# Keeping the loaded x tiles for the residual, and a new order of steps in the first part of an adaLN block

## The chip, the cores and the metric

The kernel runs on one core of a Trainium2 chip. The metric is the device time of one execution in microseconds (us), lower is better. A core has a matrix engine (TensorE, PE in the profile), a vector engine (VectorE, DVE), a scalar engine (ScalarE, ACT), a general engine (GpSimd, POOL) and a sync engine (SyncE, SP), which here does nothing but issue DMAs. Each engine works through its own queue of instructions in order; semaphores tie the queues together. Products are made in PSUM, everything else lies in SBUF.

## The reference, cut to what matters

```python
mod = (silu(c) @ wmod).reshape(2, 6, 1, 512)          # c: (2, 512)
sa, ca, ga, sb, cb, gb = mod[:, 0], ..., mod[:, 5]     # ga, gb: magnitude at least 0.25
h = layernorm(x) * (1 + ca) + sa                       # x: (2, 4096, 512) float32
x = x + ga * attn(h, W_qkva, gamma)                    # first part
h = layernorm(x) * (1 + cb) + sb
x = x + gb * ffn(h, w_gate, w_up, w_down)              # second part

def attn(x, W, gamma):
    xn = x / norm(x) * sqrt(512) * gamma
    q, kv, a = split(xn @ W.T, 3)                      # each (2, 4096, 512)
    y[n] = sigmoid(a[n]) * y[n-1] + kv[n]              # a scan along the tokens
    return q * y

def ffn(x, wg, wu, wd):                                # Q: blockwise FP4 quantize and dequantize
    h = silu(Q(x) @ Q(wg).T) * (Q(x) @ Q(wu).T)        # 1408 wide
    return Q(h) @ Q(wd).T
```

## The kernel before

**Tiling.** 8192 tokens make 64 tiles of 128 rows (index `g`) and 16 blocks of 512 tokens (index `i`), four tiles to a block. The first part (the attention-like half) writes `x + ga * attn` to the output in DRAM; the second part reads it back and adds the feed-forward half.

**The first part in slots.** There are 64 working slots. Slot `slot = 4 i + e` multiplies block `i` with the 128 output channels `e` of `q`, `kv` and `a`: 3 groups of 12 matmuls (L385) into three PSUM banks; two slots' banks alternate. The order in which each engine meets the steps of a slot is written out by hand, in one loop under a manual schedule. Beside the products of slot `s`, a slot does:

- the chain of slot `s-1`'s products: `gates` (the sigmoid on ScalarE, L403, and in the kernel before the DMA load of the matching x channels, `xs`, L398), `scan` on VectorE (L410), `read_out` on VectorE (L417 copies the last column for the next block, L419 multiplies by q), `halves` (ScalarE splits the result into 16-bit halves `yh`, L426, and SyncE issues their DMA transpose to `yt`, L428);
- for slot `s-2`: `joined` (ScalarE puts the transposed halves together, L434) and `residual` (GpSimd adds `xs`, L441, and issues the store, L443);
- the norm of x tiles ahead: the load of tile `s+7` (L328), the moments and `rstd` of tile `s+6` (L151, L156, L158, and the power on GpSimd, L159), center, shift, square and gain of tile `s+5` (L163, L169, L346, L351, L353), and the rounding into a high and a low half of tile `s+4` (`norm_hi`, L359, on ScalarE, and `norm_lo`, L364, on VectorE) with the DMA transpose into `xT` (L368), of which the next block's products are made;
- one or two units of the feed-forward weights: in the maxima slots (`max`, `maxd`, about slots 6 to 22) two block maxima with small steps (L145, L467, L472, L473); then one `finish`, in which GpSimd reduces the maxima over all partitions (L477) and VectorE takes the reciprocal (L478); then in 34 quantizing slots one unit, the generator `quant`, whose steps `advance(0)` to `advance(6)` are spread over the slot (L101, L107, L109, L120, L123, L125, L127 on VectorE, L103, L113, L116, L118 on ScalarE, and a transpose issued by SyncE).

The tiles named `ld` (8 buffers) hold loaded x tiles and loaded weight rows; center and shift work in place in them.

**Around it.** Before the slots, `start()` loads the modulation and projection weights; slots 0 to 3 also prepare the projection weights. From slot 58 on, four tiles of the first part's result are loaded (L557) and the first two are normed and quantized for the second part (`stats_x`, `quant_x`). The second part (L838, L853, L858, L888 and the same `quant`) begins when the last slot's products are through.

Of the kernel before, what the change touches and what calls it, by code (L numbers as in the profile page):

```python
# [8 lines left out]
F32 = mybir.dt.float32  # L9
F16 = mybir.dt.float16  # L10
BF16 = mybir.dt.bfloat16
U16 = mybir.dt.uint16
# [9 lines left out]
B = 2  # L22
# [22 lines left out]
def tile_adaln_block(  # L45
# [108 lines left out]
    def mean_rstd(st):  # L154
        mv = small.tile([P, 2], F32, name="mv", tag="mv", bufs=5)
        V.bn_aggr(mv, st)  # L156
        rstd = small.tile([P, 1], F32, name="rstd", tag="rstd", bufs=5)
        V.tensor_scalar(rstd, mv[:, 1:2], 1e-5, None, ALU.add)  # L158
        G.tensor_tensor(rstd, rstd, mhalf[:, 0:1], ALU.pow)  # L159
        return mv[:, 0:1], rstd  # L160

    def center(xt, mean, scale):
        V.scalar_tensor_tensor(  # L163
            out=xt, in0=xt, scalar=mean, in1=scale, op0=ALU.subtract, op1=ALU.mult
        )
        return xt

    def shift(h, rstd, by):
        V.scalar_tensor_tensor(out=h, in0=h, scalar=rstd, in1=by, op0=ALU.mult, op1=ALU.add)  # L169
# [2 lines left out]
        return work.tile([P, 2, D], F16, name="hl", tag="hl", bufs=4)  # L172

    def load_tile():
        return work.tile([P, D], F32, name="ld", tag="ld", bufs=8)


    pa = ExitStack()
# [71 lines left out]
        )  # L250

    def mod_store(s, pm):
        row = apool.tile([B, D], F32, name="row", tag="sig", bufs=2)
        if s == 5:
            signed_floor(row, pm, apool.tile([B, D], F32, name="mag", tag="y", bufs=3))
        else:
            A.activation(row, pm, AF.Copy, bias=1.0 if s in (1, 4) else 0.0)
        G.dma_start(modd[s], row)
# [61 lines left out]

    PARTS = (2, 1, 0)

    xld, xstat, xh = {}, {}, {}

    def norm_load(g):
        xld[g] = load_tile()
        b, t0 = divmod(g * P, N)
        S.dma_start(xld[g], x[b, t0 : t0 + P, :])  # L328

    def norm_moments(g):  # L330
        xstat[g] = moments(xld[g])

    def norm_stats(g):
        xstat[g] = mean_rstd(xstat[g])

    def norm_center(g):
        xh[g] = center(xld.pop(g), xstat[g][0], ca[g * P // N])

    def norm_shift(g):
        shift(xh[g], xstat.pop(g)[1], sa[g * P // N])  # L340
# [5 lines left out]
        A.activation(sq, h, AF.Square, accum_out=ss)  # L346
        xh[g] = h, ss

    def norm_gain(g):
        h, ss = xh[g]  # L350
        V.tensor_scalar(ss, ss, 1e-24, 1.0 / (D * XGAIN * XGAIN), ALU.max, ALU.mult)  # L351
        rn = small.tile([P, 1], F32, name="rn", tag="rn")
        G.tensor_tensor(rn, ss, mhalf[:, 0:1], ALU.pow)  # L353
        xh[g] = h, rn
# [38 lines left out]
        return i, e, ps  # L393

    def gates(i, e, ps):
        b, t0 = divmod(i * TB, N)
        xs = apool.tile([P, KC, P], F32, name="xs", tag="xs", bufs=3)
        S.dma_start(  # L398
            xs,
            x[b, t0 : t0 + TB, e * P : (e + 1) * P].rearrange("(t p) d -> p t d", p=P),  # L400
        )
        sig = apool.tile([P, TB], F32, name="sig", tag="sig", bufs=2)
        A.activation(sig, ps[0], AF.Sigmoid, scale=us[:, e, 2:3])  # L403
        return i, e, ps, xs, sig

    def scan(i, e, ps, xs, sig):
        b = i // BPB
        y = apool.tile([P, TB], F32, name="y", tag="y", bufs=3)
        init = 0.0 if i % BPB == 0 else carry[e]
        V.tensor_tensor_scan(out=y, data0=sig, data1=ps[1], initial=init, op0=ALU.mult, op1=ALU.add)  # L410
        return i, e, ps, xs, y

    def read_out(i, e, ps, xs, y):
        b = i // BPB
        if i % BPB != BPB - 1:
            cy = small.tile([P, 1], F32, name="cy", tag="cy", bufs=8)
            V.tensor_copy(cy, y[:, TB - 1 : TB])  # L417
            carry[e] = cy
        V.scalar_tensor_tensor(  # L419
            out=y, in0=ps[2], scalar=gq[:, e, b : b + 1], in1=y, op0=ALU.mult, op1=ALU.mult  # L420
        )
        return i, e, xs, y

    def halves(i, e, xs, y):
        yh = apool.tile([P, 2, TB], U16, name="yh", tag="yh", bufs=2)
        A.copy(yh, y.bitcast(U16).rearrange("p (t h) -> p h t", h=2))  # L426
        yt = apool.tile([P, 2, KC, P], U16, name="yt", tag="yt", bufs=2)
        S.dma_start_transpose(  # L428
            yt.rearrange("p h t e -> p (h t) e"), yh.rearrange("p h t -> p (h t)")
        )  # L430
        return i, e, xs, y, yt

    def joined(i, e, xs, y, yt):
        A.copy(  # L434
            y.bitcast(U16).rearrange("p (t e h) -> p t e h", t=KC, h=2),
            yt.rearrange("p h t e -> p t e h"),
        )
        return i, e, xs, y

    def residual(i, e, xs, y):  # L440
        G.tensor_tensor(xs, xs, y.rearrange("p (t e) -> p t e", t=KC), ALU.add)  # L441
        b, t0 = divmod(i * TB, N)
        G.dma_start(  # L443
            out[b, t0 : t0 + TB, e * P : (e + 1) * P].rearrange("(t p) d -> p t d", p=P), xs
        )
# [275 lines left out]
        mod_store(*r0)  # L721

    units, coming = [], []
    gate = joining = rows = None
    NS = NBLK * KC
    plan = [[]] * (KC + 1) + plan
    order = tc.manual_schedule(engines={V.engine, A.engine, G.engine, S.engine, T.engine})
    with order:
        xT = new_xT()
        start()  # L730
        for slot in range(NS + 2):
            i, e = divmod(slot, KC)
            if e == 0 and slot < NS:
                if slot:
                    xT = nxT
                nxT = new_xT() if i + 1 < NBLK else None
# [12 lines left out]
            if 0 < slot < 3:  # L749
                for part in PARTS:  # L750
                    hi_qkva(slot + 1, part, False)
                    lo_qkva(slot + 1, part)
            if gate is not None:
                gate = gates(*gate)
            for u in units:
                u.advance(0)
            if g < NT:
                norm_hi(g)
            if slot < 2:
                for part in PARTS:  # L760
                    gamma_qkva(slot + 2, part)
                    square_qkva(slot + 2, part)
            if gate is not None:
                gate = scan(*gate)
            for u in units:
                u.advance(1)
            if g + 1 < NT:
                norm_center(g + 1)
            if slot == 1:
                signed_floor(gq, cols, atile([P, KC, B], F32, "mag"))  # L770
                prep_gain(0)
            if gate is not None:
                gate = read_out(*gate)
            if g < NT:
                norm_lo(g, nxT)
            if g + 1 < NT:
                norm_shift(g + 1)
            for u in units:
                u.advance(2)
            if joining is not None:  # L780
                residual(*joined(*joining))
            joining = halves(*gate) if gate is not None else None
            if g + 1 < NT:
                norm_square(g + 1)
            for u in units:
                u.advance(3)
            if g + 2 < NT:
                norm_moments(g + 2)
            for u in units:
                u.advance(4)  # L790
            if g + 2 < NT:
                norm_stats(g + 2)
            for u in units:
                u.advance(5)
            if g + 1 < NT:
                norm_gain(g + 1)
            for u in units:
                u.advance(6)
            if slot < 2:
                scale_qkva(slot + 2)  # L800
            if 0 < slot < KC:
                prep_gain(slot)
            if i == 0 and e < 3:
                load_mod(3 + e)
            if late is not None:
                mod_store(*late)
            if slot == KC + 1:
                ca[1] = mod_load(1, 1, "mod_c1")
# [193 lines left out]
```

## Time and profile before

| | |
|---|---|
| median of 3 runs | 1994.95 us (1994.4 to 1995.38) |
| the profiled execution's own time | 1995.35 us |
| its span in the profile | 1993.6 us |
| busy PE, DVE | 1924.2 us (97%), 1669.2 us (84%) |
| busy ACT, POOL | 986.3 us (49%), 352.3 us (18%) |
| projection matmuls (L385), first to last | 29.0 to 609.4 us |
| residual add (L441) | 64 times, mean 1437 ns |
| second loads of x (`xs`) | 64 of 256 KB |

The profile is of one execution. Lines such as L169 are lines of the kernel before. A line of the timeline has the start in us, the duration in us, the engine, the line, the operation, what it writes and reads with shapes, and in brackets how long the engine was idle before it and what ended that. Neighbouring VectorE records overlap by some 0.08 us, so the distance of two starts is the better measure of what an instruction costs.

### The profile page before, as it was taken

What the parts mean: (1) busy time and instruction counts of PE and PEld (TensorE: products, weight loads), DVE (VectorE), ACT (ScalarE), POOL (GpSimd) and SP (SyncE); (2) the same over time, 40 slices, a digit from 0 to 9 for tenths busy, and PEclk for the clock granted to TensorE, in tenths of its full rate; (3) what the DMA queues carried; (4) which work ended last, traced back from release to release, by engine and by line L of the source; (5) the groups of instructions that cost most, each with busy time, mean ns of one, the idle gap of its engine ahead of it and who ended that gap; (6) DMA issues with size and microseconds to landing.
All of it is one profiled execution on the core that took longest, in us unless ns stands there. A gap on an engine that the chain in (4) does not pass through costs nothing.

```text
span 1993.6 us, 25757 instructions
## 1 busy us (share of the span) xinstructions
PE 1924.2 (97%) x9253; PEld 908.9 (46%) x9253; DVE 1669.2 (84%) x2851; ACT 986.3 (49%) x1648; POOL 352.3 (18%) x479
## 2 busy tenths in 40 slices
PE   7999979899989999999999999999999999999997
PEld 4344434344334444444444444444444444444444
DVE  5799979999965998888888888888888888888873
ACT  4444456666664554444444444444444444444431
POOL 4433334333331110000000000000000000000000
PEclk8999989999999999999999999999999999999999
DMA  8898879989963343433433433433533533433423
GB/s 246 210 240 217 197 167 218 209 207 205 206 166 78 67 88 68 82 65 66 83 65 66 83 65 76 83 66 70 81 69 62 85 66 64 84 67 62 80 46 50
DMA packets 516640, 222.98 MB, mean 112 GB/s; under 512 B 440470, under 2 KB 474518, under 8 KB 516512
## 3 DMA queue, kind: packets, MB, share of 16 engines
q1 hardware_dynamic: 501872, 187.76, 43.4%
q0 software_dynamic: 14640, 33.58, 9.7%
q8 instruction: 72, 1.18, 0.2%
q14 instruction: 56, 0.46, 0.1%
HBM read 79.43 MB, written 33.57 MB: 57 GB/s over the span
## 4 chain that ended last, share of the span: by engine, by line
PE 67%; DVE 19%; issue 7%; DMA 3%; POOL 1%; ACT 1%; SPq 0%; DVEq 0%; POOLq 0%; ACTq 0%
PE mm L838 41%; PE sd L888 21%; PE mm L385 4%; DVE ld L169 3%; DVE y L410 2%; DVE hl L364 2%; DVE ld L163 1%; DVE st L151 1%; DMA scratch<-in_L_wmod_dram 1%; DVE xn L120 1%; DVE hl L123 1%; DVE xn L107 1%; DVE y L419 1%; DMA yt<-yh 1%; DMA xT<-hl 1%
## 5 line engine op out<-in xcount | busy, mean ns | idle before, releaser
L838 PEld LDWEIGHTS <-x2T 128*128 128x128 f16 x4608 | 450.9, 98 | 470.5 <-issue 2.2
L385 PE MATMUL mm<-xT,wqT 128*128 128x512 f16 (+1 forms) x2412 | 516.0, 377 | 43.4 <-DMA xT<-hl 36.3
L838 PE MATMUL mm<-wuT,x2T 128*128 128x512 f16 (+1 forms) x2304 | 487.7, 361 | 2.0 <-DVE hid L858 2.0
L838 PE MATMUL mm<-wgT,x2T 128*128 128x512 f16 (+1 forms) x2304 | 487.7, 361 | 0.0
L888 PE MATMUL sd<-wdT,hT 128*128 128x512 f16 (+1 forms) x2145 | 469.0, 378 | 5.0 <-DMA hT<-hhl 5.0
L385 PEld LDWEIGHTS <-wqT 128*128 128x128 f16 x2412 | 232.7, 99 | 328.3 <-issue 72.8
L888 PEld LDWEIGHTS <-hT 128*128 128x128 f16 x2145 | 211.2, 99 | 246.3 <-DMA hT<-hhl 5.5
L853 ACT ACTIVATE silu<-mm,u 128x512 f32<-128x512 f32 (+1 forms) x192 | 124.9, 650 | 293.1 <-PE mm L838 292.9
L858 DVE SCALAR_TENSOR_TENSOR hid<-mm,u,silu 128x512 f32<-128x512 f32 (+1 forms) x192 | 128.5, 672 | 147.0 <-PE mm L838 137.1
L569 POOL TENSOR_SCALAR rstd<-vs 128x1 f32<-128x1 f32 x64 | 14.3, 224 | 984.7 <-ACT sq L567 984.7
L141 ACT ACTIVATE u<-ud,rms 128x1 f32<-128x1 f32 x64 | 18.9, 295 | 278.4 <-DVE rms L137 278.4
L113 ACT ACTIVATE she<-sh 128x512 bf16<-128x512 bf16 (+2 forms) x162 | 148.7, 918 | 4.1
L118 ACT ACTIVATE sle<-sl 128x512 f16<-128x512 f32 (+2 forms) x162 | 147.0, 907 | 0.0
L441 POOL TENSOR_TENSOR xs<-xs,y 128x512 f32<-128x512 f32 x64 | 91.9, 1437 | 207.5 <-ACT y L434 207.5
L359 ACT ACTIVATE hl<-ld,rn 128x512 f16<-128x512 f32 x64 | 46.2, 722 | 132.7 <-POOL rn L353 131.8
L911 POOL DMA_DIRECT2D out_dram<-o x65 | 57.3, 881 | 282.6 <-DVE o L908 278.8
L120 DVE SCALAR_TENSOR_TENSOR xn<-hid,xn 128x1408 f32<-128x1408 f32 x64 | 103.6, 1618 | 3.7 <-ACT hid L116 3.7
L107 DVE TENSOR_TENSOR xn<-hid,inv 128x1408 f32<-128x1408 f32 x64 | 104.0, 1625 | 2.2
L123 DVE SCALAR_TENSOR_TENSOR hhl<-hid,xn 128x1408 f16<-128x1408 f32 x64 | 104.0, 1625 | 2.2
L145 DVE TENSOR_REDUCE amh<-hid 128x88 f32<-128x1408 f32 x64 | 103.7, 1620 | 2.2
L116 ACT ACTIVATE hid<-xn 128x1408 f32<-128x1408 f32 x64 | 88.2, 1378 | 30.9 <-DVE xn L107 30.9
L169 DVE SCALAR_TENSOR_TENSOR ld<-ld,rstd,mod 128x512 f32<-128x512 f32 x96 | 96.2, 1002 | 6.8 <-DVE ld L577 0.5
(109 smaller groups left out, 1887.6 us busy)
## 6 DMA issues: line engine op xcount, KB each, us to landing
ld<-in_L_attn_x_dram SPq DMA_DIRECT2D x64, 256.0 KB, 3.7
xs<-in_L_attn_x_dram SPq DMA_DIRECT2D x64, 256.0 KB, 4.0
out_dram<-xs POOLq DMA_DIRECT2D x64, 256.0 KB, 4.4
ld<-out_dram SPq DMA_DIRECT2D x64, 256.0 KB, 2.9
out_dram<-o POOLq DMA_DIRECT2D x63, 256.0 KB, 3.9
ld<-in_L_ffn_w_gate_dram SPq DMA_DIRECT2D x22, 256.0 KB, 4.3
ld<-in_L_ffn_w_up_dram SPq DMA_DIRECT2D x22, 256.0 KB, 3.7
scratch<-in_L_wmod_dram SPq DMA_DIRECT2D x4, 1024.0 KB, 6.1
```

The source lines that it names most:

```text
L107: V.tensor_tensor(blocks(xn), blocks(src), spread(inv, nb), ALU.mult)
L113: A.activation(blocks(she), spread(sh, nb), AF.Copy, scale=WPEAK)
L118: A.activation(blocks(sle), spread(sl, nb), AF.Copy, scale=WPEAK)
L120: V.scalar_tensor_tensor(out=xn, in0=a, scalar=FLOOR, in1=xn, op0=ALU.max, op1=ALU.add)
L123: V.scalar_tensor_tensor(out=nq, in0=a, scalar=FLOOR, in1=xn, op0=ALU.max, op1=ALU.subtract)
L145: V.tensor_reduce(am, src.rearrange("p (b k) -> p b k", k=QB), AX.X, ALU.max, apply_absolute_value=True)
L169: V.scalar_tensor_tensor(out=h, in0=h, scalar=rstd, in1=by, op0=ALU.mult, op1=ALU.add)
L385: T.matmul(pp[:, t : t + width], wqT[:, wp * KC + k, r * P : (r + 1) * P], xT[:, xp * KC + k, t : t + width], start=n == 0, stop=n == 3 * ...
L838: T.matmul(pp[:, : n1 - n0], x2T[:, xp * KC + k, :], wt[:, wp * KC + k, n0:n1], start=n == 0, stop=n == 3 * KC - 1,)
L853: A.activation(sl[:, :w], pairs[j][0][:, :w], AF.Silu, scale=u[:, 0:1])
L858: V.scalar_tensor_tensor(out=hid[:, n0:n1], in0=pairs[j][1][:, : n1 - n0], scalar=u[:, 1:2], in1=sl[:, : n1 - n0], op0=ALU.mult, op1=ALU.mult,
L888: T.matmul(pd, hT[:, hp * IC + k, :], wdT[:, wd_chunk(wp, k), d : d + width], start=n == 0, stop=n == 3 * IC - 1,)
```

## The change

The loaded x tiles go into a buffer of their own, one tile `xr` for the four x tiles of a block (4 buffers), and stay there: center writes its result into a fresh `ld` tile (7 buffers instead of 8), and the residual adds the result into a slice of `xr` and stores that. The second load of x goes. `sig` and `yh` have one buffer instead of two. The addition ahead of the power for `rstd`, and in the slots the step L351 of `norm_gain`, move from VectorE to GpSimd; the copy of the last column moves from VectorE to ScalarE. `joined` and `residual` come one slot later and at the head of the slot, ahead of scan and read-out in program order; `halves` follows the read-out at once; moments and `rstd` come before the weight unit's `advance(1)`; center, shift, square and gain stand together after `advance(2)`, and `advance(3)` to `advance(6)` follow them without a break. One more slot drains the queue of joined results.

```diff
-        V.tensor_scalar(rstd, mv[:, 1:2], 1e-5, None, ALU.add)
+        G.tensor_scalar(rstd, mv[:, 1:2], 1e-5, None, ALU.add)
...
     def center(xt, mean, scale):
+        h = load_tile()
         V.scalar_tensor_tensor(
-            out=xt, in0=xt, scalar=mean, in1=scale, op0=ALU.subtract, op1=ALU.mult
-        )
-        return xt
+            out=h, in0=xt, scalar=mean, in1=scale, op0=ALU.subtract, op1=ALU.mult
+        )
+        return h
...
-        return work.tile([P, D], F32, name="ld", tag="ld", bufs=8)
+        return work.tile([P, D], F32, name="ld", tag="ld", bufs=7)
...
     def norm_load(g):
-        xld[g] = load_tile()
+        i, t = divmod(g, KC)
+        if i not in xrows:
+            xrows[i] = apool.tile([P, KC, D], F32, name="xr", tag="xr", bufs=4)
+        xld[g] = xrows[i][:, t, :]
...
-    def norm_gain(g):
+    def norm_gain(g, engine=V):
         h, ss = xh[g]
-        V.tensor_scalar(ss, ss, 1e-24, 1.0 / (D * XGAIN * XGAIN), ALU.max, ALU.mult)
+        engine.tensor_scalar(ss, ss, 1e-24, 1.0 / (D * XGAIN * XGAIN), ALU.max, ALU.mult)
...
     def gates(i, e, ps):
-        xs = apool.tile([P, KC, P], F32, name="xs", tag="xs", bufs=3)
-        S.dma_start(
-            xs,
-            x[b, t0 : t0 + TB, e * P : (e + 1) * P].rearrange("(t p) d -> p t d", p=P),
-        )
-        sig = apool.tile([P, TB], F32, name="sig", tag="sig", bufs=2)
+        sig = apool.tile([P, TB], F32, name="sig", tag="sig", bufs=1)
...
-            V.tensor_copy(cy, y[:, TB - 1 : TB])
+            A.copy(cy, y[:, TB - 1 : TB])
...
-        yh = apool.tile([P, 2, TB], U16, name="yh", tag="yh", bufs=2)
+        yh = apool.tile([P, 2, TB], U16, name="yh", tag="yh", bufs=1)
...
-    def residual(i, e, xs, y):
+    def residual(i, e, y):
+        xs = xrows[i][:, :, e * P : (e + 1) * P]
         G.tensor_tensor(xs, xs, y.rearrange("p (t e) -> p t e", t=KC), ALU.add)
...
-        for slot in range(NS + 2):
+        for slot in range(NS + 3):
...
                 u.advance(0)
+            if len(joining) == 2 or slot >= NS + 2:
+                residual(*joined(*joining.pop(0)))
             if g < NT:
                 norm_hi(g)
...
                 gate = scan(*gate)
-            for u in units:
-                u.advance(1)
-            if g + 1 < NT:
-                norm_center(g + 1)
...
-                gate = read_out(*gate)
+                joining.append(halves(*read_out(*gate)))
+            if g + 2 < NT:
+                norm_moments(g + 2)
+                norm_stats(g + 2)
+            for u in units:
+                u.advance(1)
             if g < NT:
                 norm_lo(g, nxT)
-            if g + 1 < NT:
-                norm_shift(g + 1)
             for u in units:
                 u.advance(2)
-            if joining is not None:
-                residual(*joined(*joining))
-            joining = halves(*gate) if gate is not None else None
             if g + 1 < NT:
+                norm_center(g + 1)
+                norm_shift(g + 1)
                 norm_square(g + 1)
-            for u in units:
-                u.advance(3)
-            if g + 2 < NT:
-                norm_moments(g + 2)
-            for u in units:
-                u.advance(4)
-            if g + 2 < NT:
-                norm_stats(g + 2)
-            for u in units:
-                u.advance(5)
-            if g + 1 < NT:
-                norm_gain(g + 1)
-            for u in units:
-                u.advance(6)
+                norm_gain(g + 1, G)
+            for n in range(3, 7):
+                for u in units:
+                    u.advance(n)
```

More of the change, by code (lines that the diff above doesn't have):

```diff
@@ L252, in mod_store @@
     def mod_store(s, pm):
-        row = apool.tile([B, D], F32, name="row", tag="sig", bufs=2)
+        row = apool.tile([B, D], F32, name="row", tag="sig", bufs=1)
         if s == 5:
@@ L321, in tile_adaln_block @@
     PARTS = (2, 1, 0)
-    xld, xstat, xh = {}, {}, {}
+    xld, xstat, xh, xrows = {}, {}, {}, {}
     def norm_load(g):
-        xld[g] = load_tile()
+        i, t = divmod(g, KC)
+        if i not in xrows:
+            xrows[i] = apool.tile([P, KC, D], F32, name="xr", tag="xr", bufs=4)
+        xld[g] = xrows[i][:, t, :]
         b, t0 = divmod(g * P, N)
@@ L395, in gates, with scan @@
     def gates(i, e, ps):
-        b, t0 = divmod(i * TB, N)
-        xs = apool.tile([P, KC, P], F32, name="xs", tag="xs", bufs=3)
-        S.dma_start(
-            xs,
-            x[b, t0 : t0 + TB, e * P : (e + 1) * P].rearrange("(t p) d -> p t d", p=P),
-        )
-        sig = apool.tile([P, TB], F32, name="sig", tag="sig", bufs=2)
+        sig = apool.tile([P, TB], F32, name="sig", tag="sig", bufs=1)
         A.activation(sig, ps[0], AF.Sigmoid, scale=us[:, e, 2:3])
-        return i, e, ps, xs, sig
-    def scan(i, e, ps, xs, sig):
-        b = i // BPB
+        return i, e, ps, sig
+    def scan(i, e, ps, sig):
         y = apool.tile([P, TB], F32, name="y", tag="y", bufs=3)
@@ L410, in scan, with read_out @@
         V.tensor_tensor_scan(out=y, data0=sig, data1=ps[1], initial=init, op0=ALU.mult, op1=ALU.add)
-        return i, e, ps, xs, y
-    def read_out(i, e, ps, xs, y):
-        b = i // BPB
         if i % BPB != BPB - 1:
             cy = small.tile([P, 1], F32, name="cy", tag="cy", bufs=8)
-            V.tensor_copy(cy, y[:, TB - 1 : TB])
+            A.copy(cy, y[:, TB - 1 : TB])
             carry[e] = cy
+        return i, e, ps, y
+    def read_out(i, e, ps, y):
+        b = i // BPB
         V.scalar_tensor_tensor(
@@ L421, in read_out, with halves @@
         )
-        return i, e, xs, y
-    def halves(i, e, xs, y):
-        yh = apool.tile([P, 2, TB], U16, name="yh", tag="yh", bufs=2)
+        return i, e, y
+    def halves(i, e, y):
+        yh = apool.tile([P, 2, TB], U16, name="yh", tag="yh", bufs=1)
         A.copy(yh, y.bitcast(U16).rearrange("p (t h) -> p h t", h=2))
@@ L430, in halves, with joined @@
         )
-        return i, e, xs, y, yt
-    def joined(i, e, xs, y, yt):
+        return i, e, y, yt
+    def joined(i, e, y, yt):
         A.copy(
@@ L437, in joined @@
         )
-        return i, e, xs, y
-    def residual(i, e, xs, y):
+        return i, e, y
+    def residual(i, e, y):
+        xs = xrows[i][:, :, e * P : (e + 1) * P]
         G.tensor_tensor(xs, xs, y.rearrange("p (t e) -> p t e", t=KC), ALU.add)
@@ L723, in tile_adaln_block @@
     units, coming = [], []
-    gate = joining = rows = None
+    gate = rows = None
+    joining = []
     NS = NBLK * KC
```

## The prediction, made before the result was known

> **What bounds the kernel now.** I read the page's busy table and its 40 slices first (PE 97%, but that is an average), then stretches of the first part, then its DVE and POOL timelines, then the waits. The columns of the stretches are PE, PEld, DVE, ACT and POOL busy time, clock, DMA share, GB/s.
>
> ```profile
> 94.00:243.00 149.00, 144.63 (x662) 64.77 (x661) 141.32 (x313) 72.28 (x107) 58.29 (x70) 0.99 0.91 220
> 269.00:548.00 279.00, 251.83 (x1122) 111.17 (x1121) 275.00 (x539) 186.92 (x320) 109.39 (x130) 0.95 0.94 210
> ```
>
> From 94 to 243 us (norms, projections, scan, weight maxima) PE and DVE are both nearly full; from 269 to 548 us (the weights are quantized as well) DVE works 275 of 279 us and PE doesn't. A slot's 36 matmuls take 36 x 215.8 ns = 7.77 us start to start on an undisturbed PE. The DVE slot is the distance of two scans:
>
> ```profile
> 399.00 1.18 DVE L410 TENSOR_TENSOR_SCAN y<-sig,cy,mm 128x512 f32<-128x512 f32 x1
> ...
> 401.51 0.14 DVE L417 COPY cy<-y 128x1 f32<-128x1 f32 x1
> 401.75 0.75 DVE L419 SCALAR_TENSOR_TENSOR y<-mm,gq,y 128x512 f32<-128x512 f32 x1
> 402.42 0.74 DVE L364 SCALAR_TENSOR_TENSOR hl<-ld,rn,hl 128x512 f16<-128x512 f32 x1
> 403.08 1.81 DVE L169 SCALAR_TENSOR_TENSOR ld<-ld,rstd,mod 128x512 f32<-128x512 f32 x1
> ...
> 406.81 0.15 DVE L158 TENSOR_SCALAR rstd<-mv 128x1 f32<-128x1 f32 x1
> ...
> 407.94 1.18 DVE L410 TENSOR_TENSOR_SCAN y<-sig,cy,mm 128x512 f32<-128x512 f32 x1
> ```
>
> The distance is 8.94 us. The shift (L169) takes 1.81 us where its own undisturbed form takes 0.74 (minimum of the group). POOL's residual add is why:
>
> ```profile
> 403.07 1.27 POOL L441 TENSOR_TENSOR xs<-xs,y 128x512 f32<-128x512 f32 x1 [3.77 <-ACT y L434]
> 583.79 1.34 POOL L441 TENSOR_TENSOR xs<-xs,y 128x512 f32<-128x512 f32 x1 [2.70 <-ACT y L434]
> 583.92 1.27 DVE L410 TENSOR_TENSOR_SCAN y<-sig,cy,mm 128x512 f32<-128x512 f32 x1
> ```
>
> The add at 403.07 starts 10 ns before the shift, which then waits for it. The one at 583.79 overlaps a scan, and the scan keeps its 1.27 us. PE pays at the block ends (engine, waited for: us in total, times, longest), because each block's last x tile leaves DVE late:
>
> ```profile
> PE mm L385 <- DMA xT<-hl: 36.3, 13, 10.4
> ```
>
> The second part, from 609 us on, is PE-bound (1384 us of the span) and isn't touched; the first part's saving moves it forward whole.
>
> **What the Trainium skill says.** "SBUF — State Buffer", section "SBUF: two separate sides": GpSimd and VectorE share one port pair, locked for a whole instruction, against VectorE operations with two SBUF inputs. The trace agrees: shift 1.81 against 0.74 us; the scan, which has one SBUF and one PSUM input, isn't slowed. "GPSIMD Engine Reference", section "2.1 Instruction dispatch": a loadable kernel costs an IRAM load of about 6 us. The trace has 5.69 us of idle ahead of the all-reduce and 6.90 after it. "DMA: Bandwidth & Descriptors", section "Queues, rings and completion order": a ring's descriptors are consumed in order. That fits xT's transposes landing 2.9 us (median) after issue and those of yt, issued just behind, 4.6.
>
> **The change, part by part.** Start-to-start times; a DVE instruction that needs the result just before it costs about 0.12 us more, which the new order does more often. That price is from a stretch of before where they stand so:
>
> ```profile
> 581.59 0.69 DVE L120 SCALAR_TENSOR_TENSOR xn<-ld,xn 128x512 f32<-128x512 f32 x1 [0.93 <-ACT ld L116]
> 582.32 0.69 DVE L123 SCALAR_TENSOR_TENSOR hl<-ld,xn 128x512 f16<-128x512 f32 x1
> 583.12 0.43 DVE L125 TENSOR_TENSOR hl<-hl,sle 128x512 f16<-128x512 f16 x1
> 583.58 0.42 DVE L127 TENSOR_TENSOR hl<-hl,she 128x512 f16<-128x512 f16 x1
> ```
>
> 1. *Quantizing slots, DVE.* Out go rstd, gain and carry copy (0.07+0.12+0.25) and the blocked shift (1.07). New order: reciprocal 0.26, scan then dependent read-out 1.22+0.67, moments and aggregate 0.72+0.09, xn and sl 0.58+0.16, lo 0.66, center then shift 0.78+0.66, and 0.73+0.80+0.46+0.34 for the quantizer's end (the old order had work between these: 0.60+0.59+0.33+0.34). Sum 8.13, say 8.15, against a mean of 8.74 now (scan 24 at 268.9, scan 56 at 548.5 us). 32 slots give 260.8, less 3 for the narrow 384-column units, plus 3 for PE restarting slowly and read-outs waiting: 261 against 279.6. **Gain 18.6 us.**
> 2. *Maxima slots.* Old 8.60 us (157.75 to 166.36). New: 1.31+0.67+0.72+0.20+0.66+0.78+0.66 plus two units of 1.23 = 7.46, under PE's 7.77, so PE takes over. Scans 5 to 22 took 143.1 us; 17 x 7.77 = 132.1, plus 2 for a read-out that waits for the slot's last product and for the xT transposes (part 4). **Gain 9.**
> 3. *The finish slot.* The maxima's all-reduce now follows the new GpSimd steps. Shift ends 5.1 us after the scan; square 0.9, two small GpSimd steps 0.85, load 5.7, reduce 0.4, DVE's small steps 0.5: 13.5 us against 13.3. The slot after it waited for rn behind the reload (lo idle 3.74 us, slot 12.5 us). That rn is now made before the reduce, so about 8.6. **Gain 3.7.**
> 4. *The SP queue.* The yt transposes (1.24 us of issue) now stand ahead of the xT ones, so xT lands as yt did: 4.6 us after issue instead of 2.9, and waits up to 0.8 for ScalarE's halves. At PE's pace: scan at 6.8 us after its slot's start, lo done 3.6 later, 0.8+4.6 more = 15.8 against the two slots' 15.5. So 0.3 us a block in the maxima slots (counted in 2); in the DVE-bound ones a constant delay. The removed xs load frees 0.4 us of SP issue a slot and 16.8 MB of DMA; SP is waiting anyway, so I take zero, with a gain of up to 5 us if shorter queues bring xT earlier.
> 5. *GpSimd.* It gains 2 x 0.22 us a slot (L569's row) and is busy 109 of 279 us. The add: ScalarE's square, sig, sh and joined (0.9+0.67+0.31+1.15) end 3.0 us after the shift; the next scan starts 2.6 after it. The add thus runs from 0.5 to 1.8 us of the slot, beside scan and read-out, and ends 1.0 before xn, the first operation with two SBUF inputs. Behind it wait its store and the rstd steps, which nobody needs before the next slot's shift. rn is ready 0.6 us before the scan, lo needs it 3 us later.
> 6. *ScalarE.* Carry copies: 56 x at most 0.3 us (L141's row); behind each stand the halves, which wait for the read-out anyway. ScalarE's slot sums to 6.8 of 8.15 us. Abs is done 4.3 us into the slot and needed at 5.6. Zero; with that cover gone, the excess per slot.
> 7. *Buffers.* The new center tile replaces the load's use of the seven ld tiles (three per slot, freed within two); the xr tile's fourth buffer is freed two blocks ahead; sig's single buffer is freed by the scan one slot earlier, yh's by a transpose a slot old. Zero, at worst 0.3 us a slot (9 us).
> 8. *Head and end.* In the head's slot 1 the quantizer scales now wait for gain on GpSimd after the late shift: 0.5 us lost, bounds -3 and +3. Around slot 60 the x1 loads delay xT by 10 us as before, and one more drain slot works in the shadow of the second part's first products: zero, bounds -6 and +4.
>
> Sum: 18.6+9+3.7-0.5 = 30.8. The profiled execution took 1995.35 us (span 1993.6), 0.4 over the median 1994.95: 1995.35-30.8 = 1964.5, say **1964**. If PE bound all slots from 93.9 us on, the first part would end at 552 instead of 609, so 57 is the ceiling.
>
> **Rivals.**
> - *Half is handed back* (0.20): PE's restarts cost more (a first slot after a stall takes 9.4 to 10.6 instead of 7.93 us), read-outs wait for it, and the DVE slot comes to 8.5. 33 x 0.35 = 12 plus 4 at the block ends: **1980**. For it: DVE has only 0.4 us of slack towards PE. Against: gaps under 2.2 us left the clock alone.
> - *The add still collides* (0.05): if joined ends over 1.0 us late, xn waits as the shift did. About 30 slots x 0.8 = 24: **1988**. It speaks against it that ScalarE idles before square.
> - *More is gained* (0.06): freed DMA and a calm POOL bring the DVE slot to PE's, leaving the finish stall and slot 60: **1950**.
> - *Slower* (0.07): xT behind yt. Each block waits for its last tile. The gain of 31 is gone once xT lands over 31/14 = 2.2 us later than the assumed 4.6, at 6.8 (yt's maximum was 6.6). With slot 60's 10 us at each of 14 block ends: +6 x 14 = 84, **2048**; with 8 us, +48, **2012**.
> - That the change doesn't do what it says is possible only for "beside", the second rival.
>
> **How the numbers follow.** The likeliest case (0.62) has 1954 to 1974 as its own. The range 1949 to 1987 takes in the half-gain and larger-gain cases and leaves out most of the collision and all of the slower case. 0.2% is 4 us, about what a measurement of this kernel can tell from no change. Faster: 0.62+0.20+0.06 and part of the collision, 0.89; same 0.04; slower 0.07.
>
> **What would show it.** Shifts at 0.74 us throughout and adds at 1.27 to 1.35 beside scans; scan distances near 7.8 in the maxima and 8.1 to 8.2 in the quantizing slots; no lo waiting after the reload; PE's wait for xT spread over more, shorter stalls; PE's first part ending near 578. It is wrong if the quantizing slot stays above 8.5 or L120 waits for ScalarE in it.

## The result, and the profile after

| | before | after |
|---|---|---|
| median, 8 runs each | 1995.16 us (1991.95 to 1996.01) | 1987.89 us (1986.11 to 1989.8) |
| ratio, 95% interval | | 0.9964 (0.9954 to 0.9974) |
| the profiled execution's own time | 1995.35 us | 1986.11 us |
| its span | 1993.6 us | 1984.3 us |

The change makes the kernel faster, by 7.3 us in the medians and 9.2 us in the two profiled executions. The forecast was 31. The averages of the page of the kernel after hardly hint at what happened (engine, busy us, share of the span, instructions):

```profile
span 1984.3 us, 25684 instructions
PE 1920.1 (97%) x9253; PEld 907.7 (46%) x9253; DVE 1622.3 (82%) x2672; ACT 993.3 (50%) x1704; POOL 435.2 (22%) x602
```

VectorE has 47 us less work and GpSimd 83 us more, but PE's share is what it was. So I cut the first part into stages at the starts of certain scans (counted from 0, one profiled execution of each kernel), as the forecast did. The two right-hand columns are explained further below; "forecast" is what the prediction's steps give for each stage.

| stage, us | before | after | after, `row` apart | and read-out apart | forecast |
|---|---|---|---|---|---|
| start to scan 5 | 99.9 | **119.4** | 101.5 | 101.1 | 100.4 |
| scan 5 to 22 (maxima slots) | 143.1 | 132.0 | 132.2 | 132.7 | 134.1 |
| scan 22 to 24 (the finish) | 25.8 | 24.1 | 24.3 | 24.2 | 22.1 |
| scan 24 to 56 (quantizing slots) | 279.6 | 266.2 | 266.1 | 262.0 | 261.0 |
| scan 56 to PE's last product of the first part | 60.9 | 59.2 | 59.8 | 59.0 | 60.9 |
| end of the first part | 609.4 | 601.0 | 583.8 | 579.0 | 578.5 |

The stages after scan 5 gain 11.1 + 1.7 + 13.4 + 1.7 = 27.9 us; the stage before it, which was to lose 0.5, loses 19.5. The second part takes 1383.3 us instead of 1384.2.

The stretches of the kernel after that answer to the two shown of before (PE, PEld, DVE, ACT and POOL busy time, clock, DMA share, GB/s):

```profile
119.00:251.00 132.00, 128.94 (x592) 58.05 (x591) 118.63 (x250) 72.15 (x121) 75.93 (x104) 0.99 0.79 203
276.00:542.00 266.00, 246.52 (x1121) 109.73 (x1119) 249.16 (x449) 189.93 (x349) 162.35 (x196) 0.97 0.84 189
```

In the maxima slots PE is busy 129 of 132 us and VectorE only 119: PE has taken over. In the quantizing slots neither is full: VectorE has 17 us of holes in 266.

One quantizing slot shows where they are (timeline of all engines, the lines of scan, add, carry copy, read-out and shift, and the two small steps that moved to GpSimd):

```profile
392.83 1.18 DVE L407 TENSOR_TENSOR_SCAN y<-sig,cy,mm 128x512 f32<-128x512 f32 x1
393.00 1.27 POOL L439 TENSOR_TENSOR xr<-xr,y 128x512 f32<-128x512 f32 x1 [0.39 <-ACT y L431]
394.05 0.19 ACT L410 COPY cy<-y 128x1 f32<-128x1 f32 x1 [0.50 <-DVE y L407]
394.27 0.75 DVE L416 SCALAR_TENSOR_TENSOR y<-mm,gq,y 128x512 f32<-128x512 f32 x1 [0.26 <-ACT cy L410]
...
395.94 0.56 POOL L158 TENSOR_SCALAR rstd<-mv 128x1 f32<-128x1 f32 x1 [0.53 <-DVE mv L156]
...
397.94 0.75 DVE L170 SCALAR_TENSOR_TENSOR ld<-ld,rstd,mod 128x512 f32<-128x512 f32 x1
...
399.53 0.57 POOL L355 TENSOR_SCALAR ss<-ss 128x1 f32<-128x1 f32 x1 [1.86 <-ACT sq L350]
...
401.19 1.18 DVE L407 TENSOR_TENSOR_SCAN y<-sig,cy,mm 128x512 f32<-128x512 f32 x1
```

The add starts 0.17 us after the scan, takes its undisturbed 1.27, and the shift is back at 0.75. The hole is between scan and read-out: VectorE waits 0.26 us for ScalarE's copy of the last column. The waits of the kernel after up to 660 us have that too, and two lines of waits for the store of a modulation row (engine, line, waited for: us, times, longest):

```profile
PE mm L389 <- DMA xT<-hl: 23.7, 8, 9.0
...
ACT sig L401 <- DMA modd<-row: 13.6, 3, 5.8
...
DVE y L416 <- ACT cy L410: 12.3, 39, 1.3
...
ACT row L258 <- DMA modd<-row: 7.3, 1, 7.3
```

ScalarE stands for 20.9 us in four waits for the landing of a 4 KB store, `modd<-row`. Before, this was the only such line:

```profile
ACT sig L403 <- DMA modd<-row: 0.6, 1, 0.6
```

The timeline of all engines of the kernel after shows the longest of the three that hold up a sigmoid:

```profile
82.91 0.57 ACT L258 ACTIVATE row<-sd 2x512 f32<-2x512 f32 x1
...
83.92 0.64 POOL L259 DMA_DIRECT2D modd<-row  x1
...
89.27 0.69 ACT L401 ACTIVATE sig<-mm,us 128x512 f32<-128x512 f32 x1 [5.79 <-DMA modd<-row]
...
89.99 1.22 DVE L407 TENSOR_TENSOR_SCAN y<-sig,mm 128x512 f32<-128x512 f32 x1 [7.54 <-ACT sig L401]
```

A row of the modulation is written, GpSimd issues its store, and the sigmoid of a slot, which has nothing to do with that row, starts 5.35 us after the issue. The scan behind it waits 7.54 us, and so do all slots of the head: slot 5's first matmul starts at 108.6 us, before at 93.9. Part of this is PE's clock: after a stall of 4.66 us the granted clock was 0.52 from 97 to 104 us, and slot 4's products took 10.5 us (98.1 to 108.6) instead of 7.8. Before, it was 1.00 from 80 to 100 us.

### The profile page after: what moved, and what is told of

The parts are those of the page before. It is cut to its first block, busy times and chain, and to the rows that moved or that the text cites. A ratio compares the mean times of both kernels' runs of the same rounds, so it can differ in the third digit from the quotient of the medians.

```text
span 1984.3 us, 25684 instructions
## 1 busy us (share of the span) xinstructions
PE 1920.1 (97%) x9253; PEld 907.7 (46%) x9253; DVE 1622.3 (82%) x2672; ACT 993.3 (50%) x1704; POOL 435.2 (22%) x602
## 4 chain that ended last, share of the span: by engine, by line
PE 74%; DVE 12%; issue 8%; ACT 2%; POOL 2%; DMA 2%; SPq 1%; POOLq 0%; DVEq 0%; ACTq 0%
PE mm L827 42%; PE sd L877 21%; PE mm L389 11%; DVE y L407 1%; DVE hl L368 1%; DVE y L416 1%; DVE ld L164 1%; DVE st L151 1%; DVE xn L107 1%; DMA modd<-row 1%; DVE xn L120 1%; DVE ld L170 1%; DVE hl L123 1%; DMA xT<-hl 1%; ACT y L431 0%
## 5 line engine op out<-in xcount | busy, mean ns | idle before, releaser
L389 PE MATMUL mm<-xT,wqT 128*128 128x512 f16 (+1 forms) x2412 | 511.9, 375 | 33.6 <-DMA xT<-hl 23.7
L847 DVE SCALAR_TENSOR_TENSOR hid<-mm,u,silu 128x512 f32<-128x512 f32 (+1 forms) x192 | 128.5, 672 | 146.1 <-PE mm L827 136.9
L120 DVE SCALAR_TENSOR_TENSOR xn<-hid,xn 128x1408 f32<-128x1408 f32 x64 | 103.6, 1618 | 3.7 <-ACT hid L116 3.7
L123 DVE SCALAR_TENSOR_TENSOR hhl<-hid,xn 128x1408 f16<-128x1408 f32 x64 | 104.0, 1625 | 2.2
L423 ACT COPY yh<-y 128x1024 uint16<-128x1024 uint16 x64 | 66.9, 1045 | 70.5 <-DVE y L416 63.8
L439 POOL TENSOR_TENSOR xr<-xr,y 128x512 f32<-128x512 f32 x64 | 81.4, 1271 | 66.4 <-ACT y L431 58.3
L120 DVE SCALAR_TENSOR_TENSOR xn<-ld,xn 128x512 f32<-128x512 f32 (+1 forms) x98 | 66.9, 683 | 28.0 <-ACT ld L116 28.0
```

Of the source, the lines that this page charges most:

```text
L120: V.scalar_tensor_tensor(out=xn, in0=a, scalar=FLOOR, in1=xn, op0=ALU.max, op1=ALU.add)
L123: V.scalar_tensor_tensor(out=nq, in0=a, scalar=FLOOR, in1=xn, op0=ALU.max, op1=ALU.subtract)
L389: T.matmul(pp[:, t : t + width], wqT[:, wp * KC + k, r * P : (r + 1) * P], xT[:, xp * KC + k, t : t + width], start=n == 0, stop=n == 3 * ...
L847: V.scalar_tensor_tensor(out=hid[:, n0:n1], in0=pairs[j][1][:, : n1 - n0], scalar=u[:, 1:2], in1=sl[:, : n1 - n0], op0=ALU.mult, op1=ALU.mult,
```

## The theory, and its rivals

The code names the cause. `mod_store` stages its row under the same tag as the sigmoid's tile; the change cut that tag from two buffers to one, in both places. (The diff above shows only `gates`; the full change has the same edit in `mod_store`. The lines here are those of the kernel after.)

```python
row = apool.tile([B, D], F32, name="row", tag="sig", bufs=1)   # L254, mod_store
sig = apool.tile([P, TB], F32, name="sig", tag="sig", bufs=1)  # L400, gates
```

A tile with one buffer is free again once its last reader is through. The sigmoid's reader is the scan, a VectorE instruction; the row's reader is a DMA. So in the head, where both are in use, each waits for the other's release. **Theory:** this costs nearly the whole of the head's 19.5 us, and the carry copy the rest of what is missing: the read-out writes `y` in place, so it may not start until the copy has read `y`'s last column.

**Rivals:** the head is late because the x tiles' own buffers, the steps on GpSimd or the new order are late in it, and the row only happens to be in the way; the missing time in the quantizing slots is PE's restarts or a collision with the add. A third question is which of the pieces bring the gain: the place of the add, the steps moved to GpSimd, or the load that is gone.

## The experiments

All but the second start from the kernel after. The kernel before ran beside each; its medians there were 1995.81 us (`row` apart, read-out apart, late add, two steps back) and 1995.26 us (the other four).

**1. The row in a buffer of its own** (`e1_row`). A tile of the `ld` ring, which is idle enough in the head, takes the row; the sigmoid keeps its single buffer.

```diff
-        row = apool.tile([B, D], F32, name="row", tag="sig", bufs=1)
+        row = load_tile()[:B, :]
```

> The changed kernel with one line more: the modulation row (mod_store) lies in an ld tile instead of sharing sig's single buffer. Theory: the head lost its 14.7 us (first matmul of slot 5 at 108.6 instead of 93.9 us) because ScalarE's next sigmoid, or next row, must wait until the row's store to DRAM has landed (ScalarE idle 20.9 us in 4 waits for modd<-row). Then these waits vanish, slot 5 starts at 94 to 97 us, slot 8 has no stall, and the time is 1988 - 15 = 1973 (1969 to 1977). Rival A: the steps moved to GpSimd stand behind its gamma products in the head; then slot 5 stays near 108 and the time within 3 us of 1988. Rival B: the new order in the slot (late shift, late norm_lo) delays the weight transposes; same numbers as A.

Measured: **1969.12 us** (1967.56 to 1970.09), ratio to before 0.9866 (0.9852 to 0.9879), 18.8 us below the kernel after, at the low edge of what I had expected. Row and sigmoid now follow each other at once (timeline of all engines):

```profile
77.70 0.57 ACT L258 ACTIVATE ld<-sd 2x512 f32<-2x512 f32 x1
78.18 0.66 ACT L401 ACTIVATE sig<-mm,us 128x512 f32<-128x512 f32 x1
```

No wait for `modd` is left. The stages table gives the rest: the head comes to 101.5 us, 17.9 less than after, and every later stage agrees with the kernel after within 0.6 us. So the shared tag was the head's loss, and no other stage lost by it. The rival that the other new buffers, the GpSimd steps or the order delay the head has 1.6 us left (99.9 to 101.5), all of it together.

**2. The kernel before with this one cut** (`e2_before_one`). The count alone, without anything else of the change.

```diff
-        row = apool.tile([B, D], F32, name="row", tag="sig", bufs=2)
+        row = apool.tile([B, D], F32, name="row", tag="sig", bufs=1)
...
-        sig = apool.tile([P, TB], F32, name="sig", tag="sig", bufs=2)
+        sig = apool.tile([P, TB], F32, name="sig", tag="sig", bufs=1)
```

> The kernel before, with sig's buffers (which the modulation row shares) cut from two to one and nothing else. Theory: the same ScalarE waits for the row's store appear in its head (first matmul of slot 5 from 93.9 to about 108), and as all later slots are bound by VectorE the delay stays: 12 to 19 us above the kernel before, 2007 to 2014. Rival: the head of the changed kernel was slow through its order, and one buffer costs nothing in the old one: within 3 us of 1995.

Measured: **2010.6 us** (2008.4 to 2012.42), ratio 1.0079 (1.0065 to 1.0092): 15.3 us lost. The same two waits appear in its first part:

```profile
ACT sig L403 <- DMA modd<-row: 14.7, 3, 6.2
...
ACT row L257 <- DMA modd<-row: 7.4, 1, 7.4
```

Scan 5 comes at 113.5 us instead of 99.9, and a stall of 5.7 us of PE in slot 8 is new. Slot 5's first matmul came at 101.5 us, earlier than I had expected; the total was inside. PE's granted clock stayed at 1.00 there from 94 to 113 us, unlike in the kernel after. From both sides, then: adding the cut to the kernel before costs 15.3 us, taking it out of the kernel after brings 18.8.

**3. The read-out into another tile** (`e3_apart`, on top of 1). By then the scan has read `sig`, so the result goes there, and the carry copy's source stays untouched.

```diff
-            out=y, in0=ps[2], scalar=gq[:, e, b : b + 1], in1=y, op0=ALU.mult, op1=ALU.mult
+            out=sig, in0=ps[2], scalar=gq[:, e, b : b + 1], in1=y, op0=ALU.mult, op1=ALU.mult
...
-        A.copy(yh, y.bitcast(U16).rearrange("p (t h) -> p h t", h=2))
+        A.copy(yh, sig.bitcast(U16).rearrange("p (t h) -> p h t", h=2))
```

> As e1_row, and the read-out writes into the sig tile, which the scan has used up, instead of in place over y. Theory: in the changed kernel the in-place read-out waits for ScalarE's copy of y's last column (scan to read-out 1.44 us where there is a copy, 1.29 in the last block of a batch, where there is none). Then the quantizing slot goes from 8.35 to 8.21 us, 28 slots: 4 us below e1_row. Rival: the two follow from the scan result alone; slot and time unchanged, within 1 us of e1_row.

Measured: **1963.29 us** (1962.63 to 1964.18), ratio 0.9838 (0.9824 to 0.9851), 5.8 below experiment 1. A quantizing slot in its timeline:

```profile
414.00 1.18 DVE L407 TENSOR_TENSOR_SCAN y<-sig,cy,mm 128x512 f32<-128x512 f32 x1
415.21 0.19 ACT L410 COPY cy<-y 128x1 f32<-128x1 f32 x1 [0.50 <-DVE y L407]
415.29 0.75 DVE L416 SCALAR_TENSOR_TENSOR sig<-mm,gq,y 128x512 f32<-128x512 f32 x1
...
422.21 1.20 DVE L407 TENSOR_TENSOR_SCAN y<-sig,cy,mm 128x512 f32<-128x512 f32 x1
```

Scan to read-out is 1.29 us instead of 1.44, scan to scan 8.21 instead of 8.36. Over scans 24 to 56 that is 266.1 - 262.0 = 4.1 us; the rest of the 5.8 is spread over the head, the tail and the difference from run to run. With both waits apart, the first part ends at 579.0 us.

**4. The add later in the slot** (`e4_late`, on top of 1). `joined` and `residual` go back behind `advance(2)`, the place in the slot that they had before, so the add starts late in a slot, beside VectorE's operations on two SBUF tiles. They stay two slots behind their `halves`, as in the kernel after; in the kernel before it was one.

```diff
-            if len(joining) == 2 or slot >= NS + 2:
-                residual(*joined(*joining.pop(0)))
             if g < NT:
                 norm_hi(g)
...
                 u.advance(2)
+            if len(joining) == 3 or slot >= NS:
+                residual(*joined(*joining.pop(0)))
```

> As e1_row, but joined and the residual add go back to the late place (after advance(2), one slot after their halves). Theory: the add collides with center, shift or the quantizer's two-SBUF-input operations again, 0.6 to 1.07 us a slot on VectorE: the quantizing slots 8.9 to 9.3 instead of 8.35 (33 slots: 20 to 30 us), the maxima slots 8.1 to 8.5 instead of 7.77 (up to 10 us): 25 to 40 us above e1_row, so 1998 to 2013. Rival: the gain came from the small steps that left VectorE and the place of the add is worth little: within 4 us of e1_row.

Measured: **2014.47 us** (2014.43 to 2015.36), ratio 1.0095 (1.0082 to 1.0109): 45 us over experiment 1, more than expected. The quantizing slot is 9.30 us, and its timeline shows the collision:

```profile
400.79 0.68 DVE L120 SCALAR_TENSOR_TENSOR xn<-ld,xn 128x512 f32<-128x512 f32 x1
400.99 1.61 POOL L439 TENSOR_TENSOR xr<-xr,y 128x512 f32<-128x512 f32 x1 [1.14 <-ACT y L431]
401.50 1.64 DVE L123 SCALAR_TENSOR_TENSOR hl<-ld,xn 128x512 f16<-128x512 f32 x1
```

The add comes while L120 runs and takes 1.61 us instead of 1.27; L123 comes while the add runs and takes 1.64 instead of its 0.69. Neither is slowed evenly: each ends about when the other has finished plus its own time. This agrees with the Trainium skill, "SBUF — State Buffer", section "SBUF: two separate sides", by which whichever starts first has the shared ports for its whole instruction. The direct price is 0.95 us a slot, 30 us over 32 slots; scans 24 to 56 lost 33.3, the rest of the first part 9 and the second part 4, the last for a reason that isn't known. The rn step also stands on GpSimd behind the late add, and ScalarE's `norm_hi` waits for it, 128.5 us in all instead of 5.5 in experiment 1; what that adds was not separated.

**5. The two small steps back on VectorE** (`e5_steps`, on top of 1). Same order, but the addition for `rstd` and the gain step are VectorE's again.

```diff
-        G.tensor_scalar(rstd, mv[:, 1:2], 1e-5, None, ALU.add)
+        V.tensor_scalar(rstd, mv[:, 1:2], 1e-5, None, ALU.add)
...
-                norm_gain(g + 1, G)
+                norm_gain(g + 1)
```

> As e1_row, but the addition for rstd and the gain step (L355) are on VectorE again, at their new places. Theory: in the new order the gain step stands right behind the shift and needs ScalarE's square of it, so VectorE, in order, idles 1.0 us in every slot; with the steps themselves 1.2 to 1.3 us a slot: quantizing slots 9.5, maxima slots 8.7: 33 x 1.2 + 15 = 50 us and more above e1_row, near 2025. Rival: the steps cost what they occupied before, 0.07 + 0.12 us a slot: 7 us above e1_row, 1980.

Measured: **2067.57 us** (2064.31 to 2067.89), ratio 1.0356 (1.0342 to 1.0371): 98 us over experiment 1 for two instructions of 0.15 us a slot, and nearly twice the 50 us and more that I had expected. Its timeline:

```profile
401.97 0.75 DVE L170 SCALAR_TENSOR_TENSOR ld<-ld,rstd,mod 128x512 f32<-128x512 f32 x1
...
403.51 0.15 DVE L355 TENSOR_SCALAR ss<-ss 128x1 f32<-128x1 f32 x1 [0.79 <-ACT sq L350]
...
405.39 1.26 POOL L439 TENSOR_TENSOR xr<-xr,y 128x512 f32<-128x512 f32 x1 [0.72 <-ACT y L431]
405.48 1.45 DVE L127 TENSOR_TENSOR hl<-hl,she 128x512 f16<-128x512 f16 x1
```

In the new order the square follows the shift at once, and the gain step needs the square: on VectorE it waits 0.79 us for ScalarE, with everything of the slot behind it (0.94 us with its own time). And as VectorE is now later than ScalarE, the add, whose place is set by ScalarE, meets L127 (1.45 us instead of 0.42) rather than the scan, a collision that I had not expected. The slot goes to 10.46 us. In the order of before the step stood late and found its operand ready; there it cost 0.12 us. By that figure the move would have saved little in the old order; in the new one it keeps the wait and the collision away.

**6. The rstd addition alone back on VectorE** (`e8_rstd`, on top of 3; the line with `rstd` of the diff above).

> As e3_apart, with the addition for rstd on VectorE again, at its new place. Theory (prediction's prices): 0.07 us for the step and 0.12 for following the aggregate it needs, 0.19 in each of 33 quantizing slots: 6 us above e3_apart, 1969; nothing in the maxima slots. Rival: the step fits into a gap: within 1 us.

Measured: **1971.07 us** (1967.88 to 1972.77), ratio 0.9879 (0.9865 to 0.9892): 7.8 us over experiment 3, with a slot of 8.42 instead of 8.21. Right behind the aggregate that it needs, the step of 0.15 us adds 0.21 us to the slot. If it costs as much on top of experiment 1, which was not run, most of the 98 us in experiment 5 is the gain step's and the collision's.

**7. The second load of x put back** (`e6_load`, on top of 3), into DRAM scratch tiles that nobody reads: 64 transfers of 256 KB and their issues on SP, without their SBUF. It is a stand-in: the old load wrote to SBUF, this one writes to DRAM.

```diff
+        b, t0 = divmod(i * TB, N)
+        n = (i * KC + e) % 6
+        xs = dram.tile([P, KC, P], F32, name=f"xs_{i}_{e}", tag=f"xs{n}")
+        S.dma_start(
+            xs,
+            x[b, t0 : t0 + TB, e * P : (e + 1) * P].rearrange("(t p) d -> p t d", p=P),
+        )
```

> As e3_apart, with the second load of x issued again at its old place in SyncE's queue, into a DRAM scratch tile that nobody reads (SBUF has no room for it); it reads what the old load read and writes as much to DRAM. Theory: the load was hidden and its removal worth nothing: within 2 us of 1963. Rival: the emptier DMA queues bring xT and the rows earlier: 5 us or more above.

Measured: **1966.19 us** (1964.73 to 1966.28), ratio 0.9855 (0.9841 to 0.9868): 2.9 us over experiment 3. This lies between the two expectations, and the interval overlaps that of experiment 3 (0.9824 to 0.9851), so the time alone hardly tells the load from nothing. If these 3 us are real, they are about a tenth of the 32.5 us by which experiment 3 beats the kernel before. The waits of PE in scans 24 to 56 lean to the second expectation; the first line is experiment 3, the second this one:

```profile
PE mm L389 <- DMA xT<-hl: 9.4, 3, 7.7
PE mm L389 <- DMA xT<-hl: 18.0, 7, 9.8
```

With the load, xT lands 4.2 us (median) after its issue from 276 to 525 us, without it 3.6. Four quantizing slots of 8.6 to 9.4 us stand in this profile in which the scan or the read-out waits 0.6 to 1.2 us for PE; that of experiment 3 has one such slot. This is one execution of each.

The prices of experiments 4, 5 and 7 aren't shares of the gain. Each says what undoing one part costs while the rest stays; 45, 98 and 3 us come to far more than the 32.5 us that the whole brings without the two waits.

**8. The maxima spread by DMA** (`e7_spread`, on top of 3). The finish is the stage that stays furthest behind its forecast (24.2 us against 22.1). Here the 128x3 maxima are stored to DRAM at the finish unit's first step and loaded back to all partitions; VectorE reduces them. The all-reduce on GpSimd goes.

```diff
+        gd = dram.tile([P, 3], F32, name="gd")
+        S.dma_start(gd, gsum)
+        gr = load_tile()[:, : 3 * P]
+        S.dma_start(gr, gd.rearrange("p c -> (p c)").partition_broadcast(P))
...
-        G.partition_all_reduce(gs, gsum, P, bass_isa.ReduceOp.max)
+        V.tensor_reduce(gs, gmax.pop().rearrange("q (p c) -> q c p", c=3), AX.X, ALU.max)
```

> As e3_apart, but the maxima are spread over the partitions without GpSimd's all-reduce: SyncE stores them (128 x 3) to DRAM at the head of the finish slot and loads them broadcast to all partitions, and VectorE reduces. Theory: VectorE's 8.4 us wait in the finish slot and the late adds after the reload go, at the cost of 1.5 to 2 us of waiting for two short DMAs; the two slots take 16.5 instead of 24.2 us: 7 us below e3_apart, 1956. Rival: xT at the block ends sets the pace after it anyway: within 2 us of e3_apart.

What it removes is best seen in the kernel after (timeline of all engines):

```profile
264.93 0.38 POOL L475 PARTITION_ALL_REDUCE gs<-gsum  x1 [6.24 <-issue]
265.34 0.18 DVE L476 RECIPROCAL rwk<-gs 128x3 f32<-128x3 f32 x1 [8.43 <-POOL gs L475]
...
272.34 1.46 POOL L439 TENSOR_TENSOR xr<-xr,y 128x512 f32<-128x512 f32 x1 [7.04 <-issue]
272.71 1.64 DVE L123 SCALAR_TENSOR_TENSOR hl<-ld,xn 128x512 f16<-128x512 f32 x1
```

GpSimd runs for 0.38 us and is dead for 6.24 ahead of it and 7.04 after; VectorE waits 8.43. The add that comes out of the second gap is late and collides with L123. In the spread version's timeline:

```profile
234.45 0.33 SPq L477 DMA_DIRECT2D gd<-gsum  x1
...
237.38 0.33 SPq L479 DMA_DIRECT2D ld<-gd  x1
...
242.18 0.67 DVE L484 TENSOR_REDUCE gs<-ld 128x3 f32<-128x384 f32 x1 [2.30 <-DMA ld<-gd]
```

The two DMAs take 7.7 us from the first issue to the reduce, but most of that lies under other work; VectorE waits 2.30. Measured: **1955.15 us** (1954.55 to 1956.44), ratio 0.9801 (0.9788 to 0.9815), 8.1 below experiment 3. Scans 22 to 24 take 17.2 us instead of 24.2, and scans 24 to 56 take 260.8 instead of 262.0. This is the fastest version of the study: 32.7 us below the kernel after, 40 below the one before.

## Why the prediction was wrong, and where it was right

- **Part 7, buffers: the step that failed.** It said that sig's single buffer "is freed by the scan one slot earlier", and priced all buffers at zero, at worst 9 us. True for the sigmoid, but the change cut the count in two places, and the second user of the tag is freed by a DMA's landing. Price: 17.9 us in the head and 18.8 in the total (experiment 1). It was there to be read: the full change cuts the count in `mod_store` too.
- **Part 8, head and end:** the head was to lose 0.5 us with bounds of -3 and +3; measured 19.5. The bounds covered only the scales waiting for the gain step. Without the shared tag the head loses 1.6, within them. The end, priced at zero, gained 1.7. With the 18.8 us of the row and the 5.8 of part 6 taken off, the prediction's 30.8 come to 6.2, beside 7.3 measured.
- **Part 6, the carry copies: mis-sized.** Zero, because "behind each stand the halves, which wait for the read-out anyway". That looks at what is queued behind the copy on ScalarE and forgets the one behind it on VectorE: the read-out overwrites what the copy reads. Measured 0.15 us a slot, 4.1 over the 32 quantizing slots (28 of them have the copy), 5.8 in the medians.
- **Part 1, quantizing slots: right.** Forecast 8.15 us a slot; 8.36 with the copy's wait in it, 8.21 without (experiment 3), and 262.0 us against 261 for the stage.
- **Part 2, maxima slots: right.** Forecast PE's 7.77 us plus 2 us in all; the stage took 17 x 7.76 and gained 11.1 instead of 9. The 2 us for read-outs and transposes weren't needed.
- **Part 3, the finish: half right.** 1.7 us gained instead of 3.7. The wait for rn behind the load is gone as forecast, and the slot after the finish fell from 12.5 to 9.7 us; 8.6 was missed because the add, which comes late out of GpSimd's second gap, collides there (1.46 and 1.64 us above) and because the read-out waits 0.67 us for the copy. The finish slot itself took 14.4 us instead of 13.5: GpSimd's gap ahead of the all-reduce was 6.24 us, where 5.7 was put in, and rn was ready 0.4 us later.
- **Part 4, the SP queue: no cost.** xT landed 2.8 us (median) after its issue in the maxima slots before and 2.9 after, 3.5 and 3.6 in the quantizing slots, although the yt transposes now stand ahead of it. The assumed 4.6 didn't come; yt, now first, lands sooner (in the maxima slots 3.2 us instead of 5.3). PE's waits for xT fell from 36.3 to 23.7 us in fewer stalls (13 to 8), where the prediction looked for more and shorter ones. The slower rival, which rested on the late xT, falls with it. The 3 us of experiment 7 fit, in size and by the earlier xT, the gain of up to 5 that was left open for the removed load.
- **Part 5, the add beside scan and read-out: right,** from 0.17 to 1.44 us of the slot against 0.5 to 1.8, with no collision in the maxima and quantizing slots but for the one after the finish. Experiment 4 shows what its place is worth: 45 us. The price of the moved steps was mis-sized, without harm: 0.22 us each was taken from another line (L569), but L158 takes 0.55 us on GpSimd and L355 0.41 in the mean of the first part, and the powers behind them grew from 0.63 to 0.97 and from 0.56 to 0.67. So GpSimd has 83 us more busy time instead of some 28, and had room for it; why these steps take so long isn't known.
- **The rivals.** The measured 1988 is the number given for "the add still collides", but by accident: the adds run at 1.27 us in their place and the shifts at 0.75. "Half is handed back" is nearest in kind, yet for other reasons: the quantizing slots didn't come to 8.5. What happened was not among the cases. The slower rival has a slip: 10 us less the assumed 4.6 is 5.4 a block, so 76 us rather than 84. The remark on gaps under 2.2 us, made against the half-gain, holds as read in the trace of before: around the six stalls of 0.51 to 2.15 us at L385, from 100 us on, the granted clock stayed 1.00; those of 2.43 us and more came with a lower one (0.63 from 290 to 300 us, for one), but for one of 3.27 us.

With both unforeseen waits apart, the kernel takes 1963.29 us and its first part ends at 579.0; the prediction had 1964 and "near 578". That it fits to 1 us is partly luck: the five stages differ from the forecast by +0.7, -1.4, +2.1, +1.0 and -1.9 us, and cancel.

What stays open: of the 18.5 us between the spans of the kernel after and of experiment 1 (1984.3 and 1965.8), 17.2 lie in the first part; what made the second 1.3 shorter isn't known. Why the head still loses 1.6 us without the shared tag was not tried, nor a second buffer for `sig` with the row left in it. That the removed load brings 3 us isn't clear of noise.

## What to carry to other kernels

Where a buffer count is cut, list every tile that uses the tag and what releases each: a tile whose last reader is a DMA stays taken until that transfer has landed (here the next writer started 5.35 us after the issue), and it lends this delay to all that share the tag. Where a small step moves to another engine, look also at what on the old engine may now not overwrite the step's operand; an update in place turns a free copy into a wait. And price a small instruction by when its operand is ready in the new order, not by its busy time: the same gain step cost 0.12 us a slot at its old place and some 2 at the new one, half of it through the collision that it brought.

## What was not expected of the hardware

- A 4 KB store issued from GpSimd held its buffer 5.35 us from issue to the next writer's start. The five stores of this kind landed 1.6 to 5.2 us after issue (median 2.6) in the kernel after and 2.3 to 6.8 us (median 5.7) in the kernel before, where hardly anything waited for them. The Trainium skill, "DMA: Bandwidth & Descriptors", section "Anatomy of one DMA — SWDGE (gpsimd) path", gives a fixed cost of about 2.0 us for such a DMA, most of it the receipt of the write; only the quickest stores here come near it, and the measurement decides.
- The dead time around one all-reduce on GpSimd is 6.24 us ahead and 7.04 after, for 0.38 us of work. Two small DMAs through DRAM and a reduce of 0.67 us on VectorE did the same with 2.30 us of waiting.
- An add that finds the shared ports taken, and an operation that finds the add on them, are both delayed: 1.61 and 1.64 us in experiment 4 for 1.27 and 0.69 alone.
- A step on a 128x1 tile took 0.15 us on VectorE (L158 and L351 before) and 0.4 to 0.55 us in the mean on GpSimd (L355 and L158 after).
